# Roots of the norms used later in the order of an attention and MoE kernel, and shared products moved around the hand-over

## The chip, the cores and the metric

The kernel runs on one core of a Trainium2 chip. A core has five engines, each with its own queue of instructions, carried out in order: TensorE (PE, matrix products; its weight loads are listed as PEld), VectorE (DVE), ScalarE (ACT), GpSimd (POOL) and SyncE (SP, which here mostly issues transfers). An instruction whose input is not there stops everything behind it on its engine. The metric is the device time of one execution in microseconds.

## The reference

Eight batches of 256 tokens, 256 wide, go through attention and a mixture of experts, each with a norm before and after it and a residual. Cut to what is computed:

```python
x = x + _layernorm(_L0_attn_ref(_layernorm(x), Wq, Wk, Wv, Wo, b_out))
x = x + _layernorm(_L0_ffn_ref(_layernorm(x), w_router, wg, wu, wd, sg, su, sd))

# attention: 32 query heads and 8 key/value heads of width 8, rotary q and k
scores = einsum('bkgtd,bksd->bkgts', qg, k) / sqrt(8)        # causal
ctx    = einsum('bkgts,bksd->bkgtd', softmax(scores), v);  y = ctx @ Wo + b_out

# mixture: 8 experts of inner width 640, the best 2 of a token by sigmoid, and 2 shared ones
topk_w, topk_i = top_k(sigmoid(xt @ w_router.T), 2);  topk_w /= sum(topk_w)
out = sum over the two experts of topk_w * (silu(xt @ wg.T) * (xt @ wu.T)) @ wd.T
out = out + the same, unweighted, for the two shared experts (sg, su, sd)
```

All arithmetic is in fp32. The layer norm subtracts the mean and multiplies by `(v + 1e-05) ** -0.5`, the root of this document's title.

## The kernel before

**Two parts.** In the first part the eight batches go through norm 1, the projections, attention, the norm behind it, the residual, norm 2 and the router. In the second part the tokens, sorted by expert, are worked on in 16 blocks of 256 rows and a few of 128, each with one expert's weights (1.92 MB a block, up to three in memory at a time), and their outputs are added to a table in DRAM by indirect scatter-add. A tail then computes what is left of the shared experts for the last batch, fetches the sums and applies the last norm and residual.

**An order written out by hand.** All steps of the first part are put into a list by `at(when, step, *args)`. The time is in units of one batch, so that `b + 0.5` is the middle of batch `b`'s attention. The list is sorted by that number, and the steps are emitted in that order: `for _, _, step, args in sorted(timeline, key=lambda e: e[:2])`. So a due time says nothing of microseconds. It says which step's instructions stand ahead of which in every engine's queue.

**The steps of a batch that matter here.**

- `norm1` (line 309): on VectorE the statistics of both 128-token tiles (`moments`, lines 275 and 276: `bn_stats` and `bn_aggr`, into `mv`), then on POOL the root (`rstd`, lines 280 and 281: add the epsilon, then a power; result `r`), then on VectorE the use of it (`normed`, line 285: subtract the mean and multiply by the root; result `xn`). The step emits all three at once, so VectorE comes to `normed` as soon as the statistics are done, and stands there until POOL has finished.
- `maxima` (lines 465 to 479): on PE the scores `sc` of one token tile for a group of heads and, added to them, the causal mask; then on VectorE the row maxima, negated, `nmx`.
- `split_shift` (lines 490 and 491): the maxima are split into a high and a low part, `nhl`, on VectorE.
- `shiftT` (lines 497 to 509): PE transposes `nhl` into `pm`, VectorE copies it to `nm`, and three transfers on SP's queue write it into extra rows of the query operand `qA`. The score products that follow, with these rows, give scores already shifted by the maximum.
- `weights_of` (lines 517 to 527): the scores again, transposed (`scT`) and shifted, on PE, the exponential `ex` on ACT, and for the tiles on the diagonal the causal selection on POOL. `values` (line 545) multiplies with the values into `av`, and `softmaxed`, `contextT` and `projected` bring it to the attention's output `y` (their products are `pav`, `pcx` and `py`).
- `norm_y`, `residual`, `norm2` (lines 609 to 630): statistics of `y` are taken in `projected`. `norm_y` takes the root on POOL and applies it on VectorE. `residual` adds on POOL. `norm2` takes statistics, root and use as `norm1` does; its result `x2n` is written to DRAM as rows for the later gather (line 629).
- `tokensT`, `logits`, `first_choice`, `second_choice` (from line 640): `x2n` is transposed on PE (`px`, copied to `x2T` by ACT), the router's products (`pl`) follow, and a chain of small VectorE operations picks two experts (`chosen`, line 689).
- `places` (lines 712 to 728): products with 0/1 matrices (`place`) give each token's row in the sorted table; `scatter` (line 742) writes the records by indirect transfers.

**Filler for PE.** The shared experts need no sorting. For each batch there are ten `shared_gate_up` products (line 768, eight matrix instructions each, result `gu`; behind it an activation `th` on ACT and two VectorE operations that write `sact`) and two `shared_down` products (line 781, ten instructions for each of two tiles, result `po`; copied to `ya` and sent to DRAM by SP, line 816). They are spread over the later batches as filler. For the last batch but one, the timeline places them one by one between the last products of attention. For the last batch, three gate_ups (`PRE = 3`) stand ahead of the blocks, and the other seven and both downs stand in the tail.

**The hand-over.** `make_table` (`block_table`, lines 834 to 912) works out on VectorE which expert each block has. `fetch_records` (line 946, `of<-slots`) loads a block's records, `fetch_rows` (line 916, `xg<-rows`) gathers its rows on POOL's queue, `fetch_weights` (line 930) loads an expert's weights on SP's queue. A block's rows are transposed (`pxg`, line 959), then go through `block_gate_up` (lines 768, 970, 971) and `block_down` (line 781), and the result `yb` is added to the sums by a scatter-add on POOL's queue (line 979).

**The tail** emits the remaining shared products with the steps of the last norm between them. A dictionary `behind` says which steps follow which product; the fetch of the sums follows product number `PRE`.

Of the kernel before, what the change touches and what calls it, by code (L numbers as in the profile page):

```python
# [28 lines left out]
def attn_moe_kernel(  # L29
# [47 lines left out]
    B, T, D = x.shape  # L77
    KC = D // P
    TT = T // P
# [8 lines left out]
    ISC = IS // P  # L88
# [184 lines left out]
    def moments(mv, i, src):  # L273
        st = small.tile([P, 6], F32, tag="st", name="st")
        nc.vector.bn_stats(st, src)  # L275
        nc.vector.bn_aggr(mv[:, i, :], st)  # L276

    def rstd(mv, n):
        r = small.tile([P, n], F32, tag=f"rstd{n}", name="r")
        nc.gpsimd.tensor_scalar(r, mv[:, :, 1], EPS, None, ALU.add)  # L280
        nc.gpsimd.tensor_tensor(r, r, half[:, 0:n], ALU.pow)
        return r

    def normed(dst, src, mv, r, i):
        nc.vector.tensor_scalar(
            dst, src, mv[:, i, 0:1], r[:, i : i + 1], ALU.subtract, ALU.mult
        )
# [7 lines left out]
    def at(when, step, *args):  # L295
        timeline.append((when, len(timeline), step, args))

    held = {}
# [10 lines left out]
    def norm1(b):  # L309
        mv = small.tile([P, TT, 2], F32, tag="mv1", name=f"mv1_{b}", bufs=2)  # L310
        for tt in range(TT):
            moments(mv, tt, xs[:, b * TT + tt, :])
        r = rstd(mv, TT)
        for tt in range(TT):
            xn = work.tile([P, D], F32, tag="xn", name=f"xn{b}_{tt}")
            normed(xn, xs[:, b * TT + tt, :], mv, r, tt)
            held["xn", b, tt] = xn
# [125 lines left out]
    def maxima_of(b, tt):  # L443

        width = (tt + 1) * P
        for c in range(NS):
            per = min(512 // width, heads_in(c))
            for k0 in range(0, heads_in(c), per):
                nk = min(per, heads_in(c) - k0)
                ng = 512 // (nk * width)  # L450
                for g0 in range(0, G, ng):
                    yield c, c * J + k0, nk, g0, ng
# [154 lines left out]


    def norm_y(g):
        y, mvy = held["y", g]  # L610
        r = rstd(mvy, TT)
        for i in range(TT):
            normed(y[:, i, :], y[:, i, :], mvy, r, i)

# [4 lines left out]
    def norm2(g):  # L619
        del held["y", g]  # L620
        mv2 = small.tile([P, TT, 2], F32, tag="mv2", name=f"mv2_{g}", bufs=2)
        for i in range(TT):
            moments(mv2, i, xs[:, g * TT + i, :])
        r = rstd(mv2, TT)
        xn = shared_pool.tile([P, TT, D], F32, tag="x2n", name=f"x2n{g}")
        for i in range(TT):
            normed(xn[:, i, :], xs[:, g * TT + i, :], mv2, r, i)
        held["x2n", g] = xn
        nc.sync.dma_start(
            out=rows[g * T : (g + 1) * T, :].rearrange("(t p) d -> p t d", p=P), in_=xn  # L630
        )
# [396 lines left out]
    for i, a in enumerate((-2.2, -0.93, 0.03)):  # L1028
        at(a, clear_operands, i)
        at((-1.7, a, a)[i], set_ones, i)  # L1030
        at((-1.97, -0.96, 0.02)[i], clear_values, i)
    at(0.5, set_up_router)
    at(-2.3, norm1, 0)
    for tt in range(TT):
        at(-2, transposed, 0, tt)
        at(-1.9, project, 0, tt)
        at(-1.85, split, 0, tt, 0)
        at(-1.84, keysT, 0, tt)
        for c in range(NS):
            at(-1.84 + 0.02 * c, split, 0, tt, 2 * c + 1)  # L1040
            at(-1.84 + 0.02 * c, split, 0, tt, 2 * c + 2)
            at(-1.83 + 0.02 * c, queriesT, 0, tt, c)
    at(-1.835, keys_apart, 0)
    for b in range(B):
        if b > 0:
            at(b - 2.08, norm1, b)
            for tt in range(TT):
                a = b - 1.95 + 0.45 * tt
                at(a, transposed, b, tt)
                at(a + 0.05, project, b, tt)  # L1050
                for i in range(1 + 2 * NS):
                    at(a + 0.09 + 0.03 * i, split, b, tt, i)
                at(a + 0.22, keysT, b, tt)
                for c in range(NS):
                    at(a + 0.28 + 0.06 * c, queriesT, b, tt, c)
            at(b - 1.25, keys_apart, b)
        when = b - 0.98
        for tt in range(TT):
            for m in maxima_of(b, tt):
                at(when, maxima, b, tt, *m)  # L1060
                when += 0.032
            at(when + 0.001, split_shift, b, tt)
            at(when + 0.055, shiftT, b, tt)
        last = b == B - 1
        parts_of = [(c, t) for c in range(NC) for t in range(TT)]
        when, unit = b, 0.98 / (NC * 3 * G)
        if b == 0:
            parts_of.sort(key=lambda part: part[1])
            when, unit = -0.4, 0.04
        for c, t in parts_of:  # L1070
            if b == 0 and t > 0:
                when = max(when, 0)
            for s in range(t + 1):
                for j in range(G):
                    at(when, weights_of, b, c * G + j, s, t)
                    when += unit
                at(when + 0.05, values, b, c, s, t)
            a = when + (0.1 if last else 0.12)
            at(a, softmaxed, b, c, t)
            if c == NC - 1:  # L1080
                at(a + 0.05, contextT, b, t)
                at(a + 0.09, projected, b, t)
        a = b + (1.175 if last else 1.24)
        at(a, norm_y, b)
        for t in range(TT):
            at(a + 0.02 + 0.01 * t, residual, b, t)
        at(a + 0.07, norm2, b)
        if last:
            for t in range(TT):
                at(a + 0.145 + 0.015 * t, tokensT, b, t)  # L1090
            at(a + 0.175, logits, b)
            at(a + 0.1751, first_choice, b)
            at(a + 0.1752, second_choice, b)
            at(a + 0.225, places, b)
            at(a + 0.2251, shares, b)
            for t in range(TT):
                at(a + 0.226, scatter, b, t)
            continue
        for t in range(TT):
            at(a + 0.19 + 0.02 * t, tokensT, b, t)  # L1100
        at(a + 0.24, logits, b)
        at(a + 0.27, first_choice, b)
        at(a + 0.302, second_choice, b)
        at(a + 0.37, places, b)
        at(a + 0.375, shares, b)
        for t in range(TT):
            at(a + 0.39 + 0.03 * t, scatter, b, t)
    spans = {b: (b + 1.5, b + 2.5) for b in range(B - 4)}
    spans[B - 4] = B - 2.5, B - 1.4
    spans[B - 3] = B - 1.38, B + 0.04  # L1110
    for b, (a, z) in spans.items():
        step = (z - a) / (ISC + 2 * TT)
        for i in range(ISC):
# [3 lines left out]


    for i in range(ISC):
        at(B + (0.05 + 0.034 * i if i < ISC - 2 else 0.36 + 0.001 * i), shared_gate_up, B - 2, i)  # L1120
    at(B + 0.38, shared_down, B - 2, 0)
    at(B + 0.43, shared_down, B - 2, 1)

    def free_early():

# [23 lines left out]
    at(B + 0.45, fetch_records, 2)  # L1149


    PRE = 3
    for i in range(PRE):
        at(B + 0.9, shared_gate_up, B - 1, i)

# [37 lines left out]
    with tc.If(large > NFULL):  # L1193
# [11 lines left out]
    behind = {  # L1205
        PRE: [(fetch_sums, g) for g in (final, *range(final))],
        ISC - 2: [(third_norm, 0, full)],
# [17 lines left out]
    with tc.manual_schedule():  # L1225
        for i in range(PRE, ISC + TT):
            if i < ISC:
# [64 lines left out]
```

## Time and profile before

| | |
|---|---|
| median of 3 runs | 846.39 us (844.77 to 849.11) |
| the profiled execution's own time | 851.15 us |
| its span, first to last instruction | 849.3 us |
| mean granted clock of PE | 0.962 of full speed |
| PE busy | 775.4 us, 91% of the span |
| VectorE busy | 423.8 us, 50% |
| POOL busy | 346.4 us, 41% |
| ACT busy | 259.8 us, 31% |

In this execution attention's last `av` product starts near 505 us, the first block's transposes at 548 us, and the last block ends near 807 us. The profile's rows give a start or a total in microseconds, the engine, the line of the kernel and the operation as output<-input with its shape. In rows of the timeline the last bracket is the idle time just before, and the instruction whose end released the engine. In rows of the windows, the pair of numbers before each bracket is busy time of PE, PEld, DVE, ACT and POOL in the stretch; behind them stand the granted clock of PE, the busy share of the DMA engines and GB/s. A row of the waits gives the waiting instruction, what it waited for, and then total microseconds, number of waits and the longest.

### The profile page before, as it was taken

Reading aid. Unit: us, or ns where it says so; the run is one execution under the profiler, and the core shown is the slowest. Engines: PE = TensorE matmul, PEld = TensorE weight load, DVE = VectorE, ACT = ScalarE, POOL = GpSimd, SP = SyncE. Lnnn points to the kernel's source line nnn. Section 1 sums busy time; section 2 is a strip of 40 time slices with the busy share of each in tenths; the row PEclk is TensorE's granted clock in tenths of the full one; section 3 lists DMA queues with packets and bytes.
Section 4 is the critical chain, followed back from the end, with each engine's and each line's share of the span. In section 5 each row is a group of like instructions: output and inputs, shape, how many; then the busy total and the mean of one; then the engine's idle time right before and its main releaser. Section 6 shows DMA issues by size and latency. Waiting matters only on the chain. (4 is left out here: it accounts for less than half of the span.)

```text
span 849.3 us, 11784 instructions
## 1 busy us (share of the span) xinstructions
PE 775.4 (91%) x4041; PEld 589.9 (69%) x4041; DVE 423.8 (50%) x1172; ACT 259.8 (31%) x567; POOL 346.4 (41%) x616
## 2 busy tenths in 40 slices
PE   5889789999999999999899899589999999999973
PEld 3545456776767766766666568478888888888962
DVE  5756557567667667676655626412222222222225
ACT  3554434334334334334224322011212111112213
POOL 4567435436426436435223331443122433442213
PEclk8899879999999999999989999899999999999997
DMA  5023200000000000000000003524655657579942
GB/s 149 8 80 92 80 15 14 3 27 14 7 22 15 7 21 15 8 21 15 19 9 2 13 14 143 188 75 120 209 140 180 207 154 224 149 222 299 313 121 100
DMA packets 31906, 74.62 MB, mean 88 GB/s; under 512 B 9136, under 2 KB 26032, under 8 KB 28896
## 3 DMA queue, kind: packets, MB, share of 16 engines
q1 hardware_dynamic: 20304, 58.17, 19.3%
q0 software_dynamic: 8224, 10.03, 7.0%
q10 hardware_dynamic: 3312, 5.60, 2.3%
q8 instruction: 35, 0.57, 0.3%
q14 instruction: 31, 0.25, 0.1%
HBM read 59.36 MB, written 11.80 MB: 84 GB/s over the span
## 5 line engine op out<-in xcount | busy, mean ns | idle before, releaser
L768 PE MATMUL gu<-xgT,w 128*128 128x256 f32 (+1 forms) x840 | 166.2, 357 | 3.3 <-issue 2.3
L768 PEld LDWEIGHTS gu<-xgT,w 128*128 128x128 f32 x840 | 145.8, 192 | 21.2 <-issue 3.4
L525 ACT ACTIVATE ex<-scT 128x512 f32<-128x512 f32 x192 | 113.6, 597 | 152.8 <-PE scT L517 143.7
L768 PE MATMUL gu<-x2T,ws_sb 128*128 128x256 f32 x640 | 154.7, 389 | 5.1 <-PEq L1193 5.0
L479 DVE TENSOR_REDUCE nmx<-sc 128x2 f32<-128x512 f32 (+2 forms) x208 | 129.5, 644 | 28.2 <-PE sc L472 27.2
L768 PEld LDWEIGHTS gu<-x2T,ws_sb 128*128 128x128 f32 x640 | 121.2, 195 | 28.1 <-issue 7.0
L527 POOL TENSOR_SCALAR_AFFINE_SELECT ex<-ex 128x512 f32<-128x512 f32 x128 | 81.9, 645 | 128.3 <-ACT ex L525 128.1
L971 DVE TENSOR_TENSOR act<-sg,gu 128x256 f32<-128x256 f32 (+1 forms) x105 | 40.6, 389 | 146.1 <-ACT sg L970 133.4
L465 PE MATMUL sc<-kst,qA 96*128 96x512 f32 (+2 forms) x256 | 101.5, 428 | 1.6 <-issue 1.5
L517 PE MATMUL scT<-qA,kst 102*128 102x512 f32 x192 | 98.5, 522 | 2.0 <-DMA qA<-nm 2.0
L979 POOL DMA_INDIRECT sums<-yb,of x37 | 58.3, 1576 | 97.1 <-DVE yb L978 59.9
L970 ACT ACTIVATE sg<-gu 128x256 f32<-128x256 f32 (+1 forms) x105 | 37.5, 359 | 196.9 <-PE gu L768 179.7
L781 PE MATMUL po<-w,act 128*128 128x256 f32 x370 | 83.2, 379 | 0.0
L472 PE MATMUL sc<-mask,ident_b 128*128 128x256 bf16 (+2 forms) x256 | 74.7, 295 | 0.0
L781 PEld LDWEIGHTS po<-w,act 128*128 128x128 f32 x370 | 68.8, 190 | 8.5
L781 PE MATMUL po<-ws_sb,sact 128*128 128x256 f32 x320 | 73.7, 387 | 0.0
L916 POOL DMA_INDIRECT xg<-rows,of x39 | 37.8, 970 | 82.9 <-PE pxg L959 45.0
L781 PEld LDWEIGHTS po<-ws_sb,sact 128*128 128x128 f32 x320 | 61.3, 194 | 11.6 <-ACT ex L525 3.4
L465 PEld LDWEIGHTS sc<-kst,qA 96*128 96x128 f32 x256 | 51.8, 202 | 12.6 <-issue 4.9
L803 DVE SCALAR_TENSOR_TENSOR th<-th,gu 128x256 f32<-128x256 f32 x70 | 29.3, 418 | 59.4 <-ACT th L802 57.4
L545 PE MATMUL av<-ex,v_aug 128*32 128x512 f32 x384 | 57.3, 605 | 1.3 <-POOL ex L527 1.3
L802 ACT ACTIVATE th<-gu 128x256 f32<-128x256 f32 x70 | 26.9, 384 | 98.5 <-PE gu L768 93.2
(166 smaller groups left out, 852.6 us busy)
## 6 DMA issues: line engine op xcount, KB each, us to landing
w<-in_routed SPq DMA_DIRECT2D x23, 1920.0 KB
ws_sb<-in_shared ACTq DMA_DIRECT2D x8, 480.0 KB
xs<-in_x SPq DMA_DIRECT2D x8, 256.0 KB
rows<-x2n SPq DMA_DIRECT2D x8, 256.0 KB
acc<-sums SPq DMA_DIRECT2D x4, 512.0 KB
sums<-ya SPq DMA_DIRECT2D x14, 128.0 KB
kst<-kA SPq DMA_DIRECT2D x16, 96.0 KB
out<-acc SPq DMA_DIRECT2D x3, 512.0 KB
```

The source lines that it names most:

```text
L465: nc.tensor.matmul(sc[:, g, :, :], lhsT=qA[0:SHIFT, c * G + g0 + g, ts(tt, P)], rhs=kst[0:SHIFT, k0 : k0 + nk, 0:width], start=True, stop= ...
L472: nc.tensor.matmul(sc[:, g, :, width - P :], lhsT=ident_b, rhs=mask.unsqueeze(1).to_broadcast([P, nk, P]), start=False, stop=True,)
L479: nc.vector.tensor_reduce(nmx[:, k0 : k0 + nk, g0 : g0 + ng].rearrange("p k g -> p g k"), sc, AX.X, ALU.max, negate=True,)
L517: nc.tensor.matmul(sc, lhsT=ksts[b % 3][0:KR, kv, ts(s, P)], rhs=qAs[b % 3][0:KR, ts(kv // J, G), ts(t, P)], start=True, stop=True,)
L525: nc.scalar.activation(e, sc, AF.Exp, scale=QSCALE)
L527: nc.gpsimd.affine_select(out=e, in_=e, pattern=[[0, G], [1, P]], compare_op=ALU.is_ge, fill=0.0, base=0, channel_multiplier=-1,)
L545: nc.tensor.matmul(av[32 * j : 32 * j + 32, :], lhsT=v_aug[b % 3 * TT + s][:, c * G + j, :], rhs=e.rearrange("p g t -> p (g t)"), start=(s ...
L768: nc.tensor.matmul(gu[:, half, :], lhsT=m[:, k, ts(i, P)], rhs=xT[:, k, :], start=(k == 0), stop=(k == KC - 1),)
L781: nc.tensor.matmul(po, lhsT=act[:, k, ts(t, P)], rhs=d[:, k, :], start=(k == 0), stop=(k == ic - 1),)
L916: nc.gpsimd.indirect_dma_start(out=dst, out_offset=None, in_=src, in_offset=bass.IndirectOffsetOnAxis(ap=idx, axis=0),)
L971: nc.vector.tensor_tensor(act[:, i, :], sg, gu[:, 1, :], ALU.mult)
L979: put = nc.gpsimd.indirect_dma_start(out=sums, out_offset=bass.IndirectOffsetOnAxis(ap=of[:, t, 1:2], axis=0), in_=y, in_offset=None, comp ...
```

## The change

Four edits of the order, and no change of what is computed.

- The norms before attention, behind it and before the experts are each cut in two steps: statistics and root in one, the use of the root in another, due later: `normed1` 0.045 of a batch behind `norm1`; `normed_y` where `norm_y` was, which itself goes 0.04 ahead; `normed2` 0.055 behind `norm2`. For the last batch the last two stay together.
- `shiftT` is due 0.07 instead of 0.055 behind the batch's last maxima of the tile.
- Shared products: those of batch 5 end 0.12 earlier; of batch 6's ten gate_ups, seven instead of eight are spread over the last stretch of attention, two follow at 0.36 and the tenth at 0.43, with both downs directly behind it.
- `PRE` goes from 3 to 6: six of the last batch's ten gate_ups ahead of the first block, four in the tail.

```diff
-        r = rstd(mv, TT)
+        held["mv1", b] = mv, rstd(mv, TT)
+
+    def normed1(b):
+        mv, r = held.pop(("mv1", b))
         for tt in range(TT):
             xn = work.tile([P, D], F32, tag="xn", name=f"xn{b}_{tt}")
             normed(xn, xs[:, b * TT + tt, :], mv, r, tt)
...
     def norm_y(g):
-        y, mvy = held["y", g]
-        r = rstd(mvy, TT)
+        held["mvy", g] = rstd(held["y", g][1], TT)
+
+    def normed_y(g):
+        (y, mvy), r = held["y", g], held.pop(("mvy", g))
...
-        r = rstd(mv2, TT)
+        held["mv2", g] = mv2, rstd(mv2, TT)
+
+    def normed2(g):
+        mv2, r = held.pop(("mv2", g))
         xn = shared_pool.tile([P, TT, D], F32, tag="x2n", name=f"x2n{g}")
...
+    at(-2.3, normed1, 0)
...
             at(b - 2.08, norm1, b)
+            at(b - 2.035, normed1, b)
...
-            at(when + 0.055, shiftT, b, tt)
+            at(when + 0.07, shiftT, b, tt)
...
-        at(a, norm_y, b)
+        at(a if last else a - 0.04, norm_y, b)
+        at(a, normed_y, b)
...
         at(a + 0.07, norm2, b)
+        at(a + (0.07 if last else 0.125), normed2, b)
...
-    spans[B - 3] = B - 1.38, B + 0.04
+    spans[B - 3] = B - 1.4, B - 0.08
...
-        at(B + (0.05 + 0.034 * i if i < ISC - 2 else 0.36 + 0.001 * i), shared_gate_up, B - 2, i)
-    at(B + 0.38, shared_down, B - 2, 0)
-    at(B + 0.43, shared_down, B - 2, 1)
+        a = 0.04 + 0.036 * i if i < ISC - 3 else 0.36 if i < ISC - 1 else 0.43
+        at(B + a, shared_gate_up, B - 2, i)
+    for t in range(TT):
+        at(B + 0.43, shared_down, B - 2, t)
...
-    PRE = 3
+    PRE = 6
```

## The prediction

> **What bounds the kernel now.** I read four views, in this order: the page, the engines' waits, the busy time by windows, and the timeline at the waits found, with the chain of waits last.
>
> ```profile
> span 849.3 us, 11784 instructions
> PE 775.4 (91%) x4041; PEld 589.9 (69%) x4041; DVE 423.8 (50%) x1172; ACT 259.8 (31%) x567; POOL 346.4 (41%) x616
> PE   5889789999999999999899899589999999999973
> PEclk8899879999999999999989999899999999999997
> ...
> PE pxg L959 <- DMA xg<-rows,of: 8.1, 3, 7.1
> PE pm L497 <- DVE nhl L491: 7.7, 4, 3.1
> ...
> PE place L712 <- DVE chosen L689: 3.0, 2, 2.1
> ...
> 110.00:120.00 10.00, 7.21 (x30) 5.89 (x31) 4.94 (x10) 2.87 (x8) 3.57 (x7) 0.61 0.10 32
> 420.00:430.00 10.00, 6.93 (x26) 4.71 (x19) 4.67 (x11) 0.88 (x3) 2.82 (x5) 0.66 0.09 30
> ```
>
> PE is busy 91% of the span: time goes where it idles or runs at a lower clock. The slices show both at the start, a little past the middle, and at the end. The waits name the idle: `pm` waits for the split maximum in two stalls of 3 us. The windows around those two show the clock at 0.61 and 0.66. Between them (120 to 420 us) PE is busy 294.8 of 300 us at clock 1.00; removing work from another engine there buys nothing. The timeline of the second stall:
>
> ```profile
> 420.68 0.71 POOL L281 TENSOR_TENSOR r<-r,half 128x2 f32<-128x2 f32 x1
> ...
> 421.43 1.36 DVE L285 TENSOR_SCALAR x2n<-xs,mv,r 128x256 f32<-128x256 f32 x2 [1.14 <-POOL r L281]
> 422.71 0.68 DVE L479 TENSOR_REDUCE nmx<-sc 128x2 f32<-128x512 f32 x1
> ...
> 423.75 0.37 PE L497 MATMUL pm<-ident_r,nhl 128*64 128x128 f32 x1 [3.07 <-DVE nhl L491]
> ...
> 439.97 0.17 PE L712 MATMUL place<-chosen,before 128*128 128x8 bf16 x1 [2.11 <-DVE chosen L689]
> ...
> 531.29 0.17 PE L712 MATMUL place<-chosen,before 128*128 128x8 bf16 x1
> ...
> 566.64 0.38 ACT L970 ACTIVATE sg<-gu 128x256 f32<-128x256 f32 x1 [10.25 <-remote]
> ...
> 782.48 37.95 DMA sums<-yb,of
> ```
>
> VectorE, in order, sits 1.14 us at `x2n` until POOL's root is there, and the maximum that PE needs stands behind it. The last two lines are a stall early in the blocks, and the chain of the end: the scatter-adds, not PE, decide when the sums are fetched.
>
> **The change part by part**, against the profiled execution's 851.15 us. That is 4.76 above the median of 846.39; I take the sum as a difference and apply it to the median.
>
> *A. Roots used later, batch 0 (near 110 us).* The order of the changed program puts the last `nmx` and the split ahead of both `x2n`, and one `sc`, mask and `scT` ahead of `pm` on PE. The split then is ready near 110.5, under POOL's root (109.48 to 110.51), so the stall of 3.01 at 112.79 shrinks to about 0.3: −2.7. The trace's records put the clock at half in steps of 3.41 us, here 112.3 to 122.5, each such stretch behind PE idle of at least 2 us (idle of 1.69 and 1.41 elsewhere led to none). PE was busy about 9.7 us in it, which at full clock is 4.85 less. Ends: −2.7 (the half clock comes anyhow, from other gaps of the start) and −7.5 (all of it). I take −6: the removed stall is the nearest row, but transposes that wait for `x2n` come next.
>
> *B. The same at the last batch (420 to 505 us).* The stall of 3.07 goes, and with it the half clock of 422.9 to 429.7: twenty `po` products take 6.22 us there against 4.48 at full clock, and over the stretch some 3.0 are lost. VectorE is earlier too, so the choice of experts that `place` awaits at 439.97 moves from 439.9 to about 435.2, and the gate_up now ahead of it (1.77 us) covers the rest of 2.11; the half clock behind that wait (440.0 to 443.4, ~1.7) goes as well. That is 7.8 by 444. But one product less is left for later: seven, not eight, stand between there and the last transposes, and stretches of `av` and `pav` lose their filler (idle 1.2 to 1.5 twice, against .56, .89 and .46 now). I take −5 at the last `av`; ends −7.8 and −3.
>
> *C. `shiftT` 0.015 later, all batches.* In each batch's second tile `nm` falls behind four statistics of norm 1 on VectorE (.42+.18+.40+.18 = 1.18 us), and the three DMAs that it feeds on SP start as much later. Behind them `scT` waits; it waited once, 2.05 us at 53.78, where all is short of work, and from batch 2 on never. Nothing (cover by the queue of `sc`) to +1.8 (0.9 more idle and another 0.9 at half clock): +0.5. On SP, `rows<-x2n` moves behind one `sums<-ya` (0.33 us to issue) in batches 3 to 6; nobody reads the rows before 540 us: 0. The later `x2n` itself is costed under the rivals: in batches 1 to 6 its transposes have 1.4 us in hand (at 178.2 against `px` at 179.66).
>
> *D. Shared products between attention and blocks (505 to 568 us).* Three things in order. (1) PE has one gate_up less ahead of the last transposes, so its wait for `x2n` there, 0.83 at 521.65, grows by 1.77 to about 2.5. (2) `place` of the last batch stands behind two gate_ups, no longer behind twenty `po`: 527.2 instead of 531.29, so slots are written, records read and rows gathered about 3 us earlier; but SP now issues the third weight fetch (1.92 MB) behind the first two record loads, and it lands beside the gathers. (3) The tenth gate_up's `sact` stands on VectorE behind the whole block table (ends at 539.8 now, 536.8 then), and the first `po` needs it as its last term: PE is idle from about 533.2 to 537.7, a new gap of 4.5, at whose end the clock should be at half (1.7 to 3.4 more). Then the rest of `po` (0.5+4.5) and six gate_ups (10.6) end at 553.3, 555 to 557 with the clock. Before, `pxg` came at 548.26 after a wait of 7.1 for the gathered rows. So the first block's transposes come 5 to 8 us later, at a PE that is not stopped; before, from 552.35, gate_ups ran at half clock to 556 and then stalled about 3 us for ACT, so that six were done at 568.06. From 556 on with transposes (about 1.5) and six gate_ups (10.6): 568.1. I take +0.5; ends −3 (the gathers' gain) and +8 (all of the later start).
>
> In *D*, the Trainium skill, "TensorE: Matmul & The Clock Gate", Part 1: The HAM clock gate, says the clock falls after a whole idle window of about 3.4 us that runs free of the program. This trace differs: idle of 2.11 and 3.07 us was enough. By the page's rule the 4.5 us gap covers a whole window in 1.1 of 3.4 cases, an estimate that would make its expected price about 0.8 where the trace makes it 1.7 to 3.4.
>
> *E. Six gate_ups of the last batch ahead of the blocks, four in the tail.* In the tail PE has three fewer: 5.3 to 6 us less of 14.01 for seven, ended near 828 instead of 834.5. But `sums<-yb` ends at 820.43 and the fetch at 826.24, and the norms then run on VectorE and ACT; the sum that reads `po` comes at 839.71 by itself. So 0; ends −1 (a `sact` of 0.30 lies in that chain) and 0. Its three gate_ups ahead are counted in D. The blocks (568 to 806, PE 237.4 of 238) shift whole, and the scatter chain with the last block.
>
> Sum: −6 −5 +0.5 +0.5 +0 = −10; 846.4 − 10 = 836.4 us.
>
> **The rivals.**
> 1. *Only the last batch pays.* Near 110 us the wait moves on to `px` or `pqT` (1.69 for the keys at 106.77 speaks for it: the start lacks work on PE; against it, PE holds a `sc` and `scT` that are ready). A is then −1: 846.4 −1 −5 +0.5 +0.5 = 841.4.
> 2. *The handover eats the gain.* The ACT stall (10.25, "remote") belongs to the first block itself, so it follows the later start of 553 to 557 and its 3 us of PE wait stay, beside the 4.5 us gap and one 3.4 us step more. D +11: 846.9, no change. It decides once six gate_ups are done later than 568 by more than the 10.5 gained ahead. For it: the new gap is in the order itself. Against: 7.1 us of old wait fall away.
> 3. *Slower: the later `x2n` holds PE in batches 1 to 6.* It stands behind the split and, in 3 to 6, behind a `ya` that waits for PE. If that wait passes the 1.4 us in hand, `px` waits as it does at 476.25 (1.34), and from 2 us on the clock halves for a step. 1.5 idle and 1.7 of clock, six times, is +19: 855.4. Against: its place on PE is unchanged, and VectorE is busy 207 of 300 us.
> 4. *The tail pays too*, if `sact` and `po` delay the norms more than the chain shows: −5.3 more, 831.1.
>
> **How the numbers follow.** No change is within 0.5% (842.2 to 850.6), about what a measurement here can tell. Forecast 0.55 (own range 831 to 843), rival 1 0.12, rival 2 0.13, rival 3 0.10, rival 4 0.06, others 0.04. Faster: .52 + .07 + .02 + .06 = 0.67. Same: .03 + .05 + .04 + .01 = 0.13. Slower: rival 3, half of rival 2 (.07) and .03 = 0.20. The low end is A, B and D at their best, 846.4 − 18.3 = 828; the high end takes in rival 2 and the parts at their worst (−2.7 −3 +1.8 +8 = +4): 850.
>
> **What would show it.** A: no `pm` wait of 3 us, clock at 1.00 from 110 to 130 us. B: clock at 1.00 from 420 to 445, `place` waits under 0.5. C: `scT` waits for `qA` near 54 us up to 3 us, none after 120. D: a PE idle of 4 to 5 us inside the last `po` of batch 6 with VectorE as releaser, `pxg` waiting little, six gate_ups of the blocks done 10 us earlier than 568. E: 32 matmuls in the tail's first group, the same chain of scatter-adds. I am wrong if the handover comes out over 5 us longer, or if half-clock steps appear at places that had none.

## The result and the profile after

The changed kernel takes 835.14 us (median of 4 runs, 830.95 to 839.32) against 847.75 us for the kernel before, measured beside it. The ratio is 0.9842, with a 95% interval of 0.9809 to 0.9874. A second measurement on another occasion gave 0.9841 (0.9814 to 0.9867). The forecast was 836.4 us. The profiled execution is the fastest of the four, 830.95 us, and the one of before was among the slower of its kernel, so the two traces lie 20.1 us apart where the medians lie 12.6 apart.

From the page of the changed kernel, the span, the busy times, PE's busy tenths and its clock in 40 slices:

```profile
span 829.2 us, 11794 instructions
PE 765.7 (92%) x4041; PEld 583.0 (70%) x4041; DVE 421.3 (51%) x1172; ACT 259.8 (31%) x567; POOL 344.5 (42%) x616
...
PE   4979799999999999999999996999999999999963
...
PEclk9899999999999999999999998899999999999986
```

The 9.7 us that PE is less busy are the same instructions at a higher clock. In PE's slices, the 8 of the sixth and the two 8s past the middle are 9s now, and the clock's 7 of the sixth and its 8 past the middle are gone too. The dip at the hand-over to the blocks stays, 6 now for 5 before, and the clock is low there in two slices instead of one. The engines' waits (total, number, longest) say the same:

```profile
PE po L789 <- DVE sact L806: 4.6, 1, 4.6
PE po L789 <- DVE sact L812: 4.2, 1, 4.2
PE px L648 <- DVE x2n L285: 4.1, 4, 2.5
...
PE pm L500 <- DVE nhl L494: 1.2, 1, 1.2
...
PE place L720 <- DVE chosen L697: 0.4, 1, 0.4
```

`pm` waits 1.2 instead of 7.7 us for the split, `place` 0.4 instead of 3.0, and `pxg` no longer waits for gathered rows. New are two waits of `po` for `sact`, one in the hand-over (L812) and one in the tail (L806). The wait of the last `px` for `x2n` has grown from 0.83 to 2.5 us. The timeline at the second of the old stalls:

```profile
408.09 0.66 DVE L482 TENSOR_REDUCE nmx<-sc 128x2 f32<-128x512 f32 x1
...
408.57 0.71 POOL L281 TENSOR_TENSOR r<-r,half 128x2 f32<-128x2 f32 x1
408.67 0.17 DVE L493 CAST nhl<-nmx 128x32 fp32r<-128x32 f32 x1
...
409.20 0.23 PE L500 MATMUL pm<-ident_r,nhl 128*64 128x128 f32 x1
409.31 1.36 DVE L285 TENSOR_SCALAR x2n<-xs,mv,r 128x256 f32<-128x256 f32 x2 [0.25 <-POOL r L281]
```

The maximum and the split now run while POOL takes the root. PE reaches `pm` without a wait, and VectorE itself stands 0.25 us for the root where it stood 1.14. By windows of 10 us, at the places of the old half clock and at the hand-over:

```profile
110.00:120.00 10.00, 9.98 (x55) 6.57 (x54) 7.78 (x28) 3.49 (x8) 3.23 (x6) 1.00 0.00 0
420.00:430.00 10.00, 9.44 (x54) 5.87 (x52) 9.42 (x33) 3.52 (x7) 3.35 (x6) 1.00 0.01 2
500.00:510.00 10.00, 9.80 (x46) 8.12 (x47) 6.73 (x33) 2.45 (x7) 0.00 (x0) 0.83 0.90 344
510.00:520.00 10.00, 5.77 (x21) 4.52 (x20) 6.88 (x30) 0.81 (x1) 5.24 (x8) 0.78 0.26 89
```

The clock is at 1.00 where it was 0.61 and 0.66. (The same work comes earlier now, the second of the old stalls at 409 us; in this trace the clock is full from 28 to 502 us.) It falls to 0.83 and 0.78 at the waits of the last `px` and of `po` in the hand-over.

All profiles together give an account by stages. Each number is the time in us between two instructions that every kernel has: `pm` of the first batch, `place` of the second, `place` of the fifth, the last batch's first `px`, the second block's first `pxg` (each by its start), the end of the last block's last `po`, and the end of the span.

| kernel | `pm` to `place` 2 | to `place` 5 | to last `px` | to block 2 | to last `po` | tail |
|---|---|---|---|---|---|---|
| before | 157.1 | 186.4 | 144.2 | 53.3 | 231.9 | 42.4 |
| x2n1to4 | 157.3 | 186.3 | 143.0 | 50.0 | 231.9 | 43.4 |
| filled | 152.4 | 186.3 | 141.3 | 53.3 | 231.9 | 44.6 |
| x2n0_5 | 150.5 | 186.3 | 139.1 | 49.8 | 231.9 | 44.0 |
| x2n0_5_shift | 151.5 | 186.3 | 137.5 | 49.9 | 231.9 | 43.7 |
| norms_shift | 147.5 | 186.3 | 139.1 | 50.3 | 231.9 | 46.4 |
| shared_pre6 | 156.4 | 186.3 | 138.5 | 54.3 | 233.8 | 43.2 |
| after_no_shift | 148.5 | 186.4 | 134.7 | 62.8 | 232.1 | 47.5 |
| changed kernel | 146.0 | 186.3 | 134.5 | 53.7 | 232.2 | 43.3 |
| changed kernel again | 148.5 | 186.3 | 134.6 | 55.0 | 232.7 | 47.2 |
| gu9_early | 146.2 | 186.3 | 134.6 | 57.4 | 231.9 | 48.1 |
| gu9_mid | 147.4 | 186.4 | 134.7 | 52.5 | 233.3 | 43.8 |
| gu9_mid again | 148.3 | 186.3 | 134.6 | 48.3 | 231.9 | 47.8 |
| warm | 148.6 | 186.3 | 134.5 | 48.7 | 232.0 | 42.5 |

The middle of attention is the same in every kernel to 0.1 us: there PE sets the pace, and no order on VectorE matters. The gain is in the first and the third column. The changed kernel differs between two executions by 2.5 us in the first column and by 4 us in the tail, so a single trace tells a stage, and medians tell a kernel. In the first column the difference goes with the clock: over 80 to 110 us it is 1.00 in the execution with 146.0 and 0.89 in the one with 148.5.

### The profile page after: what moved, and what is told of

Its sections match the earlier page's. It is cut to its first block, busy times and chain, and to the rows that moved or that the text cites. A ratio compares the mean times of both kernels' runs of the same rounds, so it can differ in the third digit from the quotient of the medians.

```text
span 829.2 us, 11794 instructions
## 1 busy us (share of the span) xinstructions
PE 765.7 (92%) x4041; PEld 583.0 (70%) x4041; DVE 421.3 (51%) x1172; ACT 259.8 (31%) x567; POOL 344.5 (42%) x616
## 5 line engine op out<-in xcount | busy, mean ns | idle before, releaser
L776 PE MATMUL gu<-xgT,w 128*128 128x256 f32 (+1 forms) x840 | 164.2, 355 | 0.6 <-issue 0.3
L468 PE MATMUL sc<-kst,qA 96*128 96x512 f32 (+2 forms) x256 | 99.4, 419 | 0.8 <-issue 0.5
L520 PE MATMUL scT<-qA,kst 102*128 102x512 f32 x192 | 96.1, 508 | 1.9 <-DMA qA<-nm 1.9
L789 PE MATMUL po<-ws_sb,sact 128*128 128x256 f32 x320 | 76.8, 398 | 8.8 <-DVE sact L806 4.6
L468 PEld LDWEIGHTS sc<-kst,qA 96*128 96x128 f32 x256 | 50.3, 197 | 13.6 <-issue 3.6
```

What stands on the lines that cost most here:

```text
L468: nc.tensor.matmul(sc[:, g, :, :], lhsT=qA[0:SHIFT, c * G + g0 + g, ts(tt, P)], rhs=kst[0:SHIFT, k0 : k0 + nk, 0:width], start=True, stop= ...
L520: nc.tensor.matmul(sc, lhsT=ksts[b % 3][0:KR, kv, ts(s, P)], rhs=qAs[b % 3][0:KR, ts(kv // J, G), ts(t, P)], start=True, stop=True,)
L776: nc.tensor.matmul(gu[:, half, :], lhsT=m[:, k, ts(i, P)], rhs=xT[:, k, :], start=(k == 0), stop=(k == KC - 1),)
L789: nc.tensor.matmul(po, lhsT=act[:, k, ts(t, P)], rhs=d[:, k, :], start=(k == 0), stop=(k == ic - 1),)
```

## The experiments

The theory at the outset (theory 1): the gain is the two 3 us waits of `pm` and the half clock behind them; the shared products and `PRE` do nothing net. Its rivals: half of the gain is of the shared products (theory 2); or it is spread over all batches; or only the waits count and not the clock.

**The norms and `shiftT` alone.** The shared products and `PRE` are put back:

```diff
-    spans[B - 3] = B - 1.4, B - 0.08
+    spans[B - 3] = B - 1.38, B + 0.04
...
-        a = 0.04 + 0.036 * i if i < ISC - 3 else 0.36 if i < ISC - 1 else 0.43
-        at(B + a, shared_gate_up, B - 2, i)
-    for t in range(TT):
-        at(B + 0.43, shared_down, B - 2, t)
+        at(B + (0.05 + 0.034 * i if i < ISC - 2 else 0.36 + 0.001 * i), shared_gate_up, B - 2, i)
+    at(B + 0.38, shared_down, B - 2, 0)
+    at(B + 0.43, shared_down, B - 2, 1)
...
-    PRE = 6
+    PRE = 3
```

> The first two edits alone (the roots used later, shiftT later); shared products and PRE as before. Theory 1 (the two 3 us waits of pm and the half clock behind them are the gain, the shared products do nothing net): 8 to 12 us faster than before, no pm wait over 1.3 us, clock at 1.00 from 100 to 130 and from 410 to 430 us. Theory 2 (half of the gain is of the shared products, which fill the wait of place and shorten the tail): 4 to 6 us faster, and place of batch 5 still waits about 2 us.

Measured: 836.93 us, 0.9838 of before (0.9802 to 0.9873). That is as much as the full change gains (0.9842 and 0.9841, measured on other occasions). The longest wait of `pm` is 1.2 us, and `place` still waits 2.1 us once. Theory 2 falls.

**The shared products and `PRE` alone.** The same two pieces, put into the kernel before.

> The last two edits alone (shared products of batches 5 and 6 and PRE = 6); norms and shiftT as before. Theory 1: within 3 us of before either way, with both pm waits of 3 us there, a wait of po for sact of about 4 us in the hand-over in place of pxg's wait of 7, and the chain of scatter-adds ending the run as before. Theory 2: 5 to 7 us faster.

Measured: 846.88 us, 0.9977 (0.9957 to 0.9998), some 2 us faster. Its waits show the exchange that was expected:

```profile
PE pm L497 <- DVE nhl L491: 6.4, 4, 3.1
PE po L781 <- DVE sact L804: 4.2, 1, 4.2
PE po L781 <- DVE sact L798: 4.1, 1, 4.1
PE px L640 <- DVE x2n L285: 3.1, 2, 2.5
PE place L712 <- DVE chosen L689: 0.4, 1, 0.4
```

In the stages it gains 4.5 to 5.7 us up to the last `px` (138.5 against 143.0 and 144.2), of which one gate_up of 1.77 is only put off. It gives 4 us back by the second block (54.3 against the 50.0 of x2n1to4; the 53.3 of before holds a late ACT, of which more below).

**One norm, two batches.** In the kernel before, only `normed2` is split off, and only for the two batches whose `x2n` stood ahead of the late maxima:

```diff
-        r = rstd(mv2, TT)
+        held["mv2", g] = mv2, rstd(mv2, TT)
+
+    def normed2(g):
+        mv2, r = held.pop(("mv2", g))
...
         at(a + 0.07, norm2, b)
+        at(a + (0.125 if b in (0, 5) else 0.07), normed2, b)
```

> Only normed2 is split off, and only for batches 0 and 5, whose x2n stands ahead of the maxima behind which PE waited 3 us; all else as before. Theory 1: nearly the whole gain of the norms, 6 to 10 us faster. Rival (the gain comes from many small delays over all batches, or from shiftT): less than 4 us faster.

Measured: 836.06 us, 0.9852 (0.9824 to 0.9881), 12.6 us by the ratio to its own before, 849.33. So four VectorE instructions put later, two `x2n` in each of two places, are enough for the whole of the gain, within the interval; 6 to 10 us had been expected. The waits of `pm` fall from 7.7 us to

```profile
PE pm L497 <- DVE nhl L491: 2.1, 3, 1.2
```

The first stage falls by 6.6 us and the third by 5.1.

**The same split in the batches between.** `b in (1, 2, 3, 4)` in the same line.

> Only normed2 is split off, and only for batches 1 to 4. Theory 1: PE has other work there, so no change, within 2 us of before; px does not wait. Rival 3 of the prediction (the later x2n holds PE): 5 us slower or more, with waits of px for x2n. The other rival (gain from all batches): 4 us faster or more.

Measured: 847.16 us, 0.9986 (0.9964 to 1.0008): no change. `px` waits 2.2 us in all, as before. Neither a spread gain nor the loss of the prediction's rival 3 is there.

**The wait left, the clock kept up.** The kernel before, with products of two identity matrices on PE inside the two waits:

```diff
         pm = ps_tp.tile([2 * NH, P], F32, tag="tp", name=f"pm{b}_{tt}")
+        for _ in range(24 if (b, tt) in ((2, 0), (7, 0)) else 0):
+            nc.tensor.matmul(
+                pm, lhsT=ident_r[:, 0 : 2 * NH], rhs=ident_r, start=True, stop=True
+            )
```

> The kernel before, with 24 products of two identity matrices put on PE ahead of pm for the first tile of batches 2 and 7; their result is overwritten by pm, and the order of all else stays. They need about 2.5 us and lie in the two waits of 3 us, which stay as long. Theory 1 (half of the gain is the clock, which falls because PE was idle): 5 to 8 us faster than before although no wait of pm on the split is shortened, clock near 1.00 from 112 to 122 and from 423 to 430 us. Rival (only the waits themselves cost; the clock follows something else): no change, or slower by the extra products.

Measured: 847.59 us against 852.88 for the kernel before beside it, 0.9945 (0.9927 to 0.9964), 4.7 us by the ratio. It was faster although it does more work. Two rows of the timeline and the two windows of this kernel:

```profile
415.45 1.65 PE L498 MATMUL pm<-ident_r 128*64 128x128 f32 x24
...
418.58 0.28 PE L501 MATMUL pm<-ident_r,nhl 128*64 128x128 f32 x1 [1.49 <-DVE nhl L491]
...
110.00:120.00 10.00, 9.95 (x79) 7.70 (x78) 6.17 (x13) 4.76 (x11) 3.91 (x8) 0.94 0.10 32
420.00:430.00 10.00, 9.84 (x57) 7.07 (x57) 4.50 (x13) 3.18 (x8) 2.54 (x4) 1.00 0.06 19
```

In the last batch `pm` comes 46.2 us after the fifth batch's `place`, as in the kernel before (46.3), so no wait is shorter; the products only stand in it. The clock is 0.94 and 1.00 instead of 0.61 and 0.66 (the 0.94 is a stretch of half clock that had begun at 107.8, ahead of the wait), and the two stages fall by 4.7 and 2.9 us, beside 4.85 and 3.0 worked out from the rows of before. The half clock that idle PE brings is thus worth a good third of the gain (4.7 of 12.6 us), and it can be had without removing the idle. The rival that only the waits cost falls.

**The new wait in the hand-over.** In the changed kernel, the tenth shared gate_up is due a little earlier, so that on VectorE its `sact` stands ahead of the block table:

```diff
-        a = 0.04 + 0.036 * i if i < ISC - 3 else 0.36 if i < ISC - 1 else 0.43
+        a = 0.04 + 0.036 * i if i < ISC - 3 else 0.36 if i < ISC - 1 else 0.415
```

> The changed kernel with the tenth shared gate_up of batch 6 due at 0.415 instead of 0.43: on PE in the same place, on VectorE its sact ahead of the block table. If the wait of 4.2 us of po for sact is on the path that starts the blocks: po does not wait, no half clock there, pxg 4 to 7 us earlier, 4 to 6 us faster than the changed kernel, so 16 to 19 faster than before. If the gathered rows are late anyway: pxg waits instead, 0 to 2 us faster.

Measured: 836.13 us, 0.9819 (0.9788 to 0.9849). Against the changed kernel's 0.9842, which was measured on another occasion, this did not decide.

**The tenth gate_up with the two before it.** 0.36 in the place of 0.415.

> The changed kernel with the tenth shared gate_up at 0.36, ahead of the last batch's place. The wait of po goes too, but place, records and gathers come 1.8 us later: 2 to 6 us faster than the changed kernel, pxg waiting more than with the tenth at 0.415.

Measured: 840.3 us, 0.9864 (0.9833 to 0.9894): 2 to 6 us less than the changed kernel was expected, and 0.9864 is no less than its 0.9842. The wait of `po` in the hand-over is gone, but in its profile PE idles 8.0 us ahead of the first block's gate_ups, with ACT late twice (4.1 and 5.4 us). The next experiment shows why this does not settle it.

**The tenth gate_up at 0.415, beside the changed kernel.** Both were measured in one set:

> The changed kernel once more, beside the other three of this set, for comparison: 0.982 to 0.986 of before.

> The tenth shared gate_up's sact ahead of the block table, once more beside the changed kernel. If the wait of po for it is on the path: 2 to 4 us faster than the changed kernel here too (0.979 to 0.982 of before). If the start of the blocks is limited by something else: the same as the changed kernel.

Measured: the changed kernel 836.29 us, 0.9841 (0.9814 to 0.9867); with the tenth at 0.415, 829.46 us, 0.9772 (0.9745 to 0.9798). The intervals are apart: some 6 us, where 2 to 4 were expected. In its profile `po` runs through, and `pxg` follows without a wait. The rows are PE's timeline of this kernel:

```profile
511.56 1.97 PE L776 MATMUL gu<-x2T,ws_sb 128*128 128x256 f32 x8
513.37 0.17 PE L842 MATMUL pc<-cum,ones 128*128 128x8 bf16 x1
513.39 8.88 PE L789 MATMUL po<-ws_sb,sact 128*128 128x256 f32 x40
522.11 10.52 PE L776 MATMUL gu<-x2T,ws_sb 128*128 128x256 f32 x48
532.47 0.60 PE L967 MATMUL pxg<-ident,xg 128*128 128x128 f32 x4
```

From the last `px` to the second block it takes 48.3 us against 55.0. So the wait that the change brought into the hand-over was on the path.

The same kernel had 0.9819 and 52.5 us for that stretch in gu9_mid. The occasion tells the two apart. filled, gu9_early, gu9_mid and after_no_shift were measured together, on one chip, and ACT is late in all four of their profiles (longest waits 9.5, 5.4, 4.6 and 4.1 us); it is late in none of the eight profiles from the two other occasions and chips. The ratio to before does not take this out, for it cost the kernels unequally: some 3 us in the profile of before (53.3 against 50.0), 4.2 in gu9_mid. So gu9_early and after_no_shift are better set against gu9_mid, of their own occasion. gu9_early is 4.2 us slower than that. The changed kernel is 6.8 us slower than gu9_mid_again, so gu9_early may be some 2 us faster than the changed kernel. That is an estimate, and no run had the two side by side.

**Five transposes in the wait ahead of the last `px`.** On top of the kernel with 0.415:

```diff
         pt = ps_tp.tile([P, KC, P], F32, tag="tp", name=f"px2{g}_{i}")
+        for _ in range(5 if g == B - 1 and i == 0 else 0):
+            nc.tensor.transpose(pt[:, 0, :], ident, ident)
```

> The kernel with the tenth gate_up at 0.415, and five transposes of an identity on PE in the wait of 2.5 us ahead of the last batch's transposes (about 1 us of work, overwritten by px). If that wait brings the step at half clock near 502 us: the step goes and 1 to 2 us with it. If not: the same as the kernel without them.

Measured: 828.16 us, 0.9751 (0.9728 to 0.9773), the fastest of all, though not told apart from 0.9772. Its reason is not the one expected: the transposes end at 501.5 us, 1.91 us of wait remain behind them, and the clock still goes to half at 503.7, for 6.8 us. The stage to the second block is the same (48.7). The step of the prediction's kind was not removed, so nothing is shown on its price.

**`shiftT` put back, and `shiftT` alone.** The changed kernel with `when + 0.055`:

> The changed kernel with shiftT back at 0.055. Theory 1 (the order on VectorE decides; shiftT costs 0.5): within 2 us of the changed kernel. Rival (shiftT's later place is needed to cover the root): waits of pm for the split of 1 to 2 us come back near 105 and 409 us, 3 to 5 us slower than the changed kernel.

Measured: 843.91 us, 0.9898 (0.9871 to 0.9925), slower than the changed kernel. But the stages ahead of the last `px` are the same (148.5, 186.4, 134.7 against 148.5, 186.3, 134.6), and `pm` waits no more than 1.2 us: the rival's two waits come back, but with 0.61 and 0.55 us. The difference in its profile lies behind them (62.8 against 55.0), where ACT was late twice (4.1 and 3.3 us) and PE 6.2 us behind it; `shiftT` moves nothing there. Neither theory has that, but the occasion does: it is 7.8 us slower than gu9_mid beside it, and the changed kernel is 6.8 us slower than gu9_mid_again beside that. So `shiftT` put back costs some 1 us by this estimate, which is not told apart from nothing; the two kernels were not run side by side.

The split for batches 0 and 5, with `when + 0.07`:

> normed2 split off for batches 0 and 5 alone, and shiftT at 0.07. My prediction had shiftT at 0 to 1.8 us of loss; the traces of the kernels with and without it speak for a gain of 1 to 3 us near 90 us, because the statistics and the root of norm 1 no longer stand behind nm, so that the transposes of xn start earlier. Gain: 0.980 to 0.984 of before, clock over 80 to 110 us at 0.93 or more. Loss or nothing: 0.985 or more, clock there 0.85 to 0.89 as without it.

Measured: 838.12 us, 0.9872 (0.9841 to 0.9903), against 0.9852 without the later `shiftT` on another occasion, so no gain, and the clock over 80 to 110 us is 0.89 as in before. The wait for `qA` has grown (timeline of this kernel):

```profile
51.27 0.82 DVE L285 TENSOR_SCALAR xn<-xs,mv,r 128x256 f32<-128x256 f32 x2 [1.14 <-POOL r L281]
52.01 0.27 DVE L505 CAST nm<-pm 64x128 fp32r<-64x128 f32 x1
...
54.40 0.80 PE L517 MATMUL scT<-qA,kst 102*128 102x512 f32 x1 [3.79 <-DMA qA<-nm]
```

With norm 1 in one piece, `nm` stands behind its root and its use as well, and `scT` waits 3.79 us, where it waited 2.05 in before and 1.55 in x2n0_5. With norm 1 split it waits 1.8 to 1.9 in the changed kernel. So a later `shiftT` lengthens this wait by itself, and the split of norm 1 takes that away. Whether it makes the kernel slower is not shown: the intervals of 0.9872 and 0.9852 overlap.

## Why the prediction was right, point by point

**A, the first wait.** Right in mechanism, undersized. Taken at −6; the split of `x2n` alone took 6.6 us off the stage. But the whole change took off 8.6 to 11.1. The term that was left out is the split of norm 1, and of the norm behind attention, in the first batches: with them the stage is 146.0 to 148.6, without them 150.5 and 151.5. Which of the two norms it is was not tried. The waits showed `pxn` and `pqT` waiting there, and I costed only `x2n`.

**B, the last batch.** Taken at −5, measured −9.7 (134.5 against 144.2; −8.5 against 143.0). The norms alone bring 5.1; the rest is the gate_up ahead of `place`, which covers its wait of 2.1 us and with it the half clock behind that wait, and one gate_up put off. The step that failed is "idle 1.2 to 1.5 twice" between there and the last `av`: the filler taken from these stretches was not missed, and the clock stood at 1.00 from 420 to 460 us.

**C, `shiftT`.** The mechanism, `nm` behind the statistics and a longer wait for `qA`, is real where norm 1 is whole (3.79). In the change as it is it costs nothing, since `scT` waits 1.85 against 2.05. The estimate of +0.5 was made as if norm 1 were not split.

**D, the hand-over.** The wait of 2.5 us ahead of the last `px`, the idle of 4 to 5 us inside `po` with VectorE as releaser, half clock there, `pxg` without a wait: all four came as worked out (2.54, 4.23, the clock at 0.78, and `pxg` waiting 0.2 for ACT). Not priced was a stretch of half clock behind the wait of 2.54 (502.0 to 505.5), at a place that had none: one of the prediction's own signs of being wrong, though its rows had half clock behind every idle of 2 us or more. `place` came 7.0 us behind the last `px` instead of 9.6. The size did not come out. I set the late start of the blocks against "about 3 us" of wait for ACT that would fall away. Set against the 53.3 us of the profile from which it was worked out, +0.5 is nearly met (+0.4 to +1.7). But that ACT stall does not belong to the kernel: nine of the fourteen profiles, x2n1to4 with before's own hand-over among them, have none. Against the 50.0 us of a hand-over without the stall, the changed one takes 53.7 to 55.0: +4 to +5. Putting the tenth gate_up ahead of the table gave that back.

**E, the tail.** Right: three gate_ups fewer moved nothing. The chain of waits ends in both kernels with the scatter-adds,

```profile
761.64 38.80 DMA sums<-yb,of
...
801.11 5.04 DMA acc<-sums
```

and the tail takes 43.3 us against 42.4 (and 46.4 in norms_shift, which has three gate_ups ahead as before: the stage scatters by more than was asked of it). The fourth gate_up's `sact` now even stands behind statistics that wait for the sums, so `po` waits 4.6 us. Its products end at 815.5, and the sum that reads them comes at 819.6, 9.6 us ahead of the end as before.

**The sum.** −10 was near −12.6 because A and B were too small by 3 to 5 us each and D, against a hand-over without the stall, by 3 to 5 the other way. The mechanisms came, but that the number lies so close is in part luck. Rival 2 was half right, its idle and its half clock are there, but at +4 instead of +11; rivals 1, 3 and 4 did not occur.

**The clock rule.** I set the rule of the Trainium skill, "TensorE: Matmul & The Clock Gate", Part 1: The HAM clock gate, of a whole idle window of 3.4 us, against the rows. The rows hold: idle of 2.5 us was followed by half clock here too (502.0 us), and 24 small products kept the clock up in a wait of 3 us. But by the length of the idle alone they hold only as a likelihood. The wait of 2.1 us for `place` brought a step in the profiles of before, norms_shift, x2n0_5, x2n1to4 and filled, and none in x2n0_5_shift. Where the idle falls tells them apart. In each trace the clock changes only on a grid of 3.41 us. In the five, the 2.1 us lie in one step of the grid, and the half clock begins at its end; in x2n0_5_shift the grid parts them into 1.2 and 0.9. Over all fourteen traces, from 30 to 800 us, every step with 1.9 us of idle PE or more was followed by half clock, and no half clock began behind one with less than 1.5. This agrees with the window that runs free of the program, of which the same section of the Trainium skill speaks; that a whole window of idle is needed is not what the traces show.

## What to carry to other kernels

Where an engine works in order, give a step that needs another engine's answer its own place in the order, behind work that does not need it: splitting "ask" from "use" in two places was worth 1.5%. Look for it only where the bounding engine idles; the same edit in four batches with a full PE changed nothing. When filler is moved, follow the last term of the product that needs it through every queue: a gate_up 0.015 of a batch too late put its result behind a table of some thirty instructions, and cost about as much as the moved filler had gained.

## What was not expected of the hardware

- Idle PE costs twice: 24 products of no use in each of two waits made the kernel 4.7 us faster (0.9945), because the clock stayed up behind them.
- ACT was late by 3 to 10 us at the start of the blocks in five of the fourteen profiles, before, filled, gu9_early, gu9_mid and after_no_shift, with no releaser inside the core's program ("remote" in the rows). It goes with the occasion: all four profiles of one chip have it, and none of the eight of two other chips; on which chip before was profiled is not on record. The same order of instructions had it on the one and not on another (gu9_mid and gu9_mid_again, 52.5 and 48.3 us from the last `px` to the second block). In before it is the row of 10.25 us at 566.64 shown ahead. What it waits for is not settled, and gu9_early and after_no_shift were not tried on another chip.
- The tail took 42.4 to 48.1 us for much the same work: 43.3 and 47.2 in two executions of the changed kernel. The transfer row that leads it went from 38.80 to 42.16 us. Why was not found.
